# Second attention of a decoder layer: the norm of its own keys kept as a row of sums of squares and applied to the scores

## Chip, cores, metric

One Trainium2 chip, one core of it. The metric is the device time of one execution in microseconds (us). A TensorE matrix multiplication of 128 x 128 weights against up to 512 columns is a "matmul" here; PE is TensorE, DVE VectorE, ACT ScalarE, POOL GpSimd, and SP the engine that issues nearly all DMAs.

## What is computed

One decoder layer for 8 sequences of 100 tokens, width 1024, in fp32: a retention-style first attention, a second attention whose keys and values are those of a context of 722 rows followed by the layer's own 100 tokens, and a gated feed-forward net; a residual and a layer norm after each. What the change touches is the second attention (16 query heads, 4 key heads):

```python
q = (x @ wq).reshape(B, L, NUM_HEADS, HEAD_DIM)
k = (x @ wk).reshape(B, L, NUM_KV_HEADS, HEAD_DIM)
...
q = rms_norm(q, q_norm_w)
k = rms_norm(k, k_norm_w)
k_ctx = (h_ctx_kv @ wk_ctx).reshape(B, T, NUM_KV_HEADS, HEAD_DIM)
...
k_ctx = rms_norm(k_ctx, k_norm_w)
q = q * cos + rotate_half(q) * sin
k = k * cos + rotate_half(k) * sin
k_full = jnp.concatenate([k_ctx, k], axis=1)
...
scores = jnp.einsum('blhd,bmhd->bhlm', q, k_full) * scale + mask
probs = jax.nn.softmax(scores, axis=-1)
```

The norm of a key divides all 128 elements of it by one number, the root of their mean square. The rotation leaves the sum of squares of a key as it is. So this number may be applied to the key or to the key's row of scores.

## The kernel before

**Precision and layout.** A product in fp32 is three matmuls: each operand is split into a high and a low part, hi x hi, hi x lo, lo x hi (`mm3`, L85 to 88). `split2` (L63) makes the parts: a ScalarE copy (L67) and a VectorE subtraction (L68). Activations lie with features on the 128 partitions and tokens on the columns; a half is 4 sequences, 400 columns. `proj` (a loop over `mmw`) runs 24 matmuls of 400 columns into a bank of PSUM.

**Order.** The kernel is written as a program, and a list scheduler with a simulated time line then fixes the order of the instructions on each engine. Each engine runs its own queue in that order; an instruction whose input is not there holds all that stand behind it. That goes for SP too: a DMA that must wait for a buffer, or for another DMA's landing, holds the DMAs behind it.

**Stages** in the profile's time: first attention to about 440, its output projection to 605, the second attention's projections (L622 to 656) to 850, the attention over context and own keys (L661 to 764) to 1600, its output projection to 1730, the feed-forward net to 2450, the last norm to the end.

**The projections** go over 4 key heads, and for each over 6 units of weights (4 of queries, 1 of keys, 1 of values) and two halves. For a query or key unit: square the projection (L645), sum it over the partitions with GpSimd's all-reduce into `ss` (L125), rotate (`rope`, L133 to 137: two ScalarE copies, three VectorE operations), take the inverse root (`inv_root`: ScalarE Ln, Exp and Square at L113, L116, L118, and one Newton step on VectorE at L119 and L120, which leaves -2 times the root), multiply (L650), split into `d`, and store `d` to DRAM (`qd` or `kd`, L654). Values are turned by TensorE (`tokens_first`: a ScalarE copy `vt` at L145, the transposes at L148), split into `vs` and stored to `vd` (L642). The context keys and values of the first sequence's first two key heads are interleaved with this. The tiles `t`, `r`, `ss`, `sq` have two buffers here, `d` three.

**The attention** goes over 8 sequences and 4 key heads, 32 pairs. For each pair `context_keys` projects the 722 context rows in two parts, squares them (L604), sums them over the partitions into `ss` (tile kss, L605; its last 46 columns are set to 1 at L599), and writes that as a row to DRAM (L609). The unnormed keys, multiplied by the constant `kws` (the weight of the norm times -0.5 sqrt(128)), lie in `kall`; the 100 own keys, which are normed, are loaded behind them (L677). The row comes back from DRAM as a column, `rr` (L694: 128 partitions x 6), because the scores are laid out with keys on the partitions; six small operations (L696 to L703) make of it the factors `rk`. The scores are computed in 7 chunks of 128 keys, in the order 6, 5, 0, 1, 2, 3, 4. Chunk 6 holds own keys alone, chunk 5 82 rows of the context and 46 own keys. As each chunk leaves PSUM its rows are multiplied by a column of `rk`: chunks 0 to 4 on ScalarE (L722), chunks 5 and 6 on VectorE with the mask added (L718), where own keys have the factor 1: rows 82 to 127 of rk's column 5 are never written after the first 1.0, and chunk 6 uses the constant. Softmax, the product with the values and the store to `o2d` (L764) follow. Context values (`context_values`) are copied to `cvt` (L618) and turned by TensorE (L688).

At the change of sequence `load_context` loads the next context in 8 pieces `cs` (L588) and splits them into tiles `big`. These loads, the weights `w<-wcd` (L82), `kall`, `vall`, `q`, the row and `rr` all are issued by SP.

Of the kernel before, what the change touches and what calls it, by code (L numbers as in the profile page):

```python
# [8 lines left out]
F32 = mybir.dt.float32  # L9
FR = mybir.dt.float32r  # L10
AF = mybir.ActivationFunctionType
ALU = mybir.AluOpType
# [4 lines left out]
P = 128  # L17
B, T, D = 8, 100, 1024
# [4 lines left out]
SC, SH = 722, 362  # L23
SN = [SH, SC - SH]
NC = 7
ORDER = (6, 5, 0, 1, 2, 3, 4)
C5 = SC - 5 * P
# [4 lines left out]
NKV = 4  # L32
# [7 lines left out]
def decoder_layer(ctx, tc, xT, cT, w1, wo1, w2, wo2, wc, w3, wd, gw, qw, kw, trig, dec, mask, out):  # L40
# [18 lines left out]
    def bt(ap):  # L59
        return ap.rearrange("p (b t) -> p b t", b=NB)  # L60
# [49 lines left out]
    def inv_root(pool, ss, eps, n=N, pin=False):  # L110

        r = pool.tile([P, n], F32, tag="r0", name="r0")
        ln = nc.scalar.activation(r, ss, AF.Ln, bias=eps)  # L113
        if pin:
            tc.keep_in_program_order(ln)
        nc.scalar.activation(r, r, AF.Exp, scale=-0.5)  # L116
        q = pool.tile([P, n], F32, tag="r1", name="r1")
        nc.scalar.activation(q, r, AF.Square)  # L118
        nc.vector.scalar_tensor_tensor(q, ss, eps, q, ALU.add, ALU.mult)  # L119
        nc.vector.scalar_tensor_tensor(q, q, 3.0, r, ALU.subtract, ALU.mult)  # L120
        return q
# [31 lines left out]
    qd = dr.tile([NKV, 4, P, B, 2, T], FR, name="qd")  # L153
    kd = dr.tile([NKV, P, B, 2, T], FR, name="kd")
    vd = dr.tile([NKV, T, B, 2, P], FR, name="vd")
    o2d = dr.tile([B, P, NKV, 4, 2, T], FR, name="o2d")
    zd = dr.tile([2, P, KT, N], F32, name="zd")
    zd2 = dr.tile([2, P, KT, N], F32, name="zd2")
# [24 lines left out]
    eps_k = const(128e-6, "eps_k")  # L183
    rks = []
    for i in range(2):
        rk = cp.tile([P, 6], F32, name=f"rk{i}")
        nc.vector.memset(rk, 1.0)
        rks.append(rk)
    msk = cp.tile([P, 2, T], F32, name="msk")
    wts = cp.tile([P, 4], F32, name="wts")  # L190
    gws = cp.tile([P, 2], F32, name="gws")
# [4 lines left out]
    def load_constants(p, trg):  # L196
        dcy = p.tile([T, NH1, T], F32, name="dcy", bufs=1)
        nc.sync.dma_start(out=dcy, in_=dec)
        nc.sync.dma_start(out=msk, in_=mask)
        nc.sync.dma_start(out=wts[:, 0:2], in_=gw)  # L200
        nc.sync.dma_start(out=wts[:, 2:3], in_=qw)
        nc.sync.dma_start(out=wts[:, 3:4], in_=kw)

        nc.vector.tensor_scalar(gws, wts[:, 0:2], -8.0, None, ALU.mult)
        nc.vector.tensor_scalar(kws, wts[:, 3:4], -0.5 * math.sqrt(P), None, ALU.mult)
        nc.vector.tensor_scalar(tq, trg[:, 2:4], wts[:, 2:3], None, ALU.mult)
        nc.vector.tensor_scalar(tk, trg[:, 2:4], wts[:, 3:4], None, ALU.mult)
        for t in (tq, tk):
            sw = p.tile([P, T], F32, tag="vt", name="sw", bufs=1)
            nc.vector.tensor_copy(sw, t[:, 1])  # L210
            nc.vector.tensor_copy(t[0:P // 2, 1], sw[P // 2:P])
            nc.vector.tensor_copy(t[P // 2:P, 1], sw[0:P // 2])
        return dcy
# [361 lines left out]
    kapool = sbuf("ka", 2, "right")  # L575
    ka = kapool.__enter__()
    cz = []

    def load_context(b):

# [8 lines left out]
                split(z[k // QT][:, :, k % QT:k % QT + 2, :n], cs)  # L589
            cz.append(z)  # L590

    def context_keys(kv):

        kall = ka.tile([P, 2, SC + T], FR, tag="kall", name="kall")
        wk = load_ws(2 * kv)
        sq = ka.tile([P, SC], F32, tag="ksq", name="ksq", bufs=1)
        ss = ka.tile([P, 6 * P], F32, tag="kss", name="kss", bufs=1)
        row = dr.tile([6, P], F32, tag="row", name="row", bufs=2)
        nc.gpsimd.memset(ss[:, SC:], 1.0)  # L599

        def step(hf):
            n, at = SN[hf], slice(hf * SH, hf * SH + SN[hf])
            acc = proj(wk, cz[hf], n)
            nc.scalar.activation(sq[:, at], acc, AF.Square)  # L604
            nc.gpsimd.partition_all_reduce(ss[:, at], sq[:, at], P, RED.add)  # L605
            nc.scalar.activation(kall[:, 0, at], acc, AF.Copy, scale=kws)
            nc.vector.scalar_tensor_tensor(kall[:, 1, at], acc, kws, f32(kall[:, 0, at]), ALU.mult, ALU.subtract)
            if hf:
                nc.sync.dma_start(out=row.rearrange("c p -> (c p)")[None, :], in_=ss[0:1])  # L609
        return step, (kall, row)  # L610

    def context_values(kv):
# [10 lines left out]
    with sbuf("l2", 2) as p:  # L623
        for kv in range(NKV):
            for i0, i1 in ((0, 4), (4, 6)) if kv == 0 else ((0, 2), (2, 4), (4, 6)):
                if (kv, i0) == (0, 4):
                    load_context(0)
                ws = [load_w(w2[kv, i]) for i in range(i0, i1)]
                if (kv, i0) in ((1, 2), (2, 2)):
                    step, kept = context_keys(kv - 1)  # L630
                    early.append(kept)
                if (kv, i0) in ((1, 2), (2, 0), (2, 2), (3, 0)):
                    step(i0 == 0)
                for half in range(2):
                    bs = slice(half * NB, (half + 1) * NB)
                    for i in range(i0, i1):
                        acc = proj(ws[i - i0], z1[half], tag=acc_tag())
                        if i == 5:
                            tr = tokens_first(p, acc).rearrange("p (b d) -> p b d", b=NB)
                            vs = p.tile([T, NB, 2, P], FR, tag="vs", name="vs", bufs=1)  # L640
                            split2(vs[:, :, 0], vs[:, :, 1], tr)
                            nc.sync.dma_start(out=f32(vd[kv, :, bs]), in_=f32(vs))  # L642
                            continue
                        sq = p.tile([P, N], F32, tag="sq", name="sq")
                        nc.scalar.activation(sq, acc, AF.Square)  # L645
                        ss = all_red(p, sq, "ss")
                        tb = tq if i < 4 else tk
                        t = rope(p, acc, tb[:, 0], tb[:, 1])
                        r = inv_root(p, ss, eps_k)
                        nc.vector.scalar_tensor_tensor(  # L650
                            t, t, -0.5 if i < 4 else -0.5 * math.sqrt(P), r, ALU.mult, ALU.mult)
                        d = p.tile([P, NB, 2, T], FR, tag="d", name="d", bufs=3)
                        split2(d[:, :, 0], d[:, :, 1], bt(t))
                        nc.sync.dma_start(out=f32(qd[kv, i, :, bs] if i < 4 else kd[kv, :, bs]), in_=f32(d))  # L654
# [5 lines left out]
    with sbuf("cx", 2) as p, sbuf("c1", 1) as p1:  # L660
# [6 lines left out]
        for b in range(B):  # L667
            if b > 0:
                load_context(b)
            for kv in range(NKV):  # L670
                if early:
                    kall, row = early.pop(0)
                else:
                    step, (kall, row) = context_keys(kv)
                    step(0)
                    step(1)
                nc.sync.dma_start(out=f32(kall[:, :, SC:]), in_=f32(kd[kv, :, b]))  # L677
# [11 lines left out]
                    src = tr[0:rows, 0:(c1 - c0) * P].rearrange("p (c d) -> p c d", d=P)  # L689
                    split2(vall[0:rows, c0:c1, 0], vall[0:rows, c0:c1, 1], src)  # L690

                rr = p.tile([P, 6], F32, tag="rr", name="rr")
                with nc.allow_non_contiguous_dma("a row turned into a column"):
                    nc.sync.dma_start(out=rr, in_=row.rearrange("c p -> p c"))  # L694
                r0 = p.tile([P, 6], F32, tag="rr0", name="rr0")
                nc.scalar.activation(r0, rr, AF.Ln, bias=eps_k)  # L696
                nc.scalar.activation(r0, r0, AF.Exp, scale=-0.5)
                r1 = p.tile([P, 6], F32, tag="rr1", name="rr1")
                nc.vector.tensor_tensor(r1, r0, r0, ALU.mult)
                nc.vector.scalar_tensor_tensor(r1, rr, eps_k, r1, ALU.add, ALU.mult)  # L700
                rk = rks[kv % 2]
                nc.vector.scalar_tensor_tensor(rk[:, 0:5], r1[:, 0:5], 3.0, r0[:, 0:5], ALU.subtract, ALU.mult)
                nc.vector.scalar_tensor_tensor(rk[0:C5, 5:6], r1[0:C5, 5:6], 3.0, r0[0:C5, 5:6], ALU.subtract, ALU.mult)  # L703

                s = p1.tile([P, NC, N], F32, tag="s", name="s")
                mx = p.tile([P, N], F32, tag="mx", name="mx")
# [4 lines left out]
                for j, c in enumerate(ORDER):  # L711
                    rows, n, t0 = (R6, N6, T6) if c == 6 else (P, N, 0)
                    sp = bank("s")[0:rows, :n]
                    kh, kl = (kall[:, i, c * P:c * P + rows] for i in range(2))
                    mm3(bt(sp), kh, kl, q[:, :, 0, t0:], q[:, :, 1, t0:], True, True)
                    sc = s[0:rows, j, :n]
                    if c >= 5:
                        nc.vector.scalar_tensor_tensor(  # L718
                            bt(sc), bt(sp), rk[:, 5:6] if c == 5 else 1.0,
                            msk[0:rows, c - 5, None, t0:].to_broadcast([rows, 4, T - t0]), ALU.mult, ALU.add)  # L720
                    else:
                        nc.scalar.activation(sc, sp, AF.Copy, scale=rk[:, c:c + 1])  # L722
                        nc.vector.tensor_tensor(mx, s[:, 1] if j == 2 else mx, sc, ALU.max)
                    if j == 2:
                        m6 = part(mx, 6)
                        nc.vector.tensor_tensor(m6, m6, bt(s[0:R6, 0, :N6]), ALU.max)
# [348 lines left out]
```

## Time and profile before

| | us |
|---|---|
| median of 3 runs (lowest, highest) | 2515.79 (2514.77, 2517.98) |
| the profiled execution | 2517.7 |
| its span | 2515.9 |
| PE / DVE / ACT / POOL busy | 2465.4 / 1992.2 / 1343.5 / 481.2 |
| mean granted clock of TensorE | 0.993 of full |
| PE busy in 600 to 700, 700 to 800, 850 to 1000 | 89.72, 95.54, 149.49 |
| DVE busy in 600 to 700, 700 to 800, 850 to 1000 | 96.42, 91.33, 129.66 |
| all-reduce, one (56 in all of tile ss; 64 of tile kss) | 2.9; 2.7 |

How to read it: a busy time is the sum of an engine's instructions, the span runs from the first to the last of them. Line names such as L650 are lines of the kernel; "t<-t,r" is output and inputs by tile names. "DVE t L650" as a releaser means that a wait ended when VectorE's instruction of that line, on that tile, was done. The granted clock is what the chip's throttle lets TensorE have; at 0.5 each matmul takes twice its time.

### The profile page before, as it was taken

The numbers are of one execution on the slowest core, as the hardware profiler recorded it, in microseconds if no ns is written. First come the engines' busy times: TensorE is split into PE (matmuls) and PEld (weight loads), VectorE is DVE, ScalarE is ACT, GpSimd is POOL, SyncE is SP. The second block draws the span as 40 slices with busy tenths as digits, with TensorE's granted clock in tenths as the row PEclk, the third lists the DMA queues.
The fourth block names the chain that finished last, engine by engine and source line by source line (L and its number), as shares of the span: only waits on it lengthen the run. The fifth ranks groups of instructions, "written<-read, shape, count | busy, mean of one in ns | idle before, by whom it ended". The sixth has DMA issues, their size and how long they took to land.

```text
span 2515.9 us, 37158 instructions
## 1 busy us (share of the span) xinstructions
PE 2465.4 (98%) x14036; PEld 2442.0 (97%) x14036; DVE 1992.2 (79%) x3110; ACT 1343.5 (53%) x2264; POOL 481.2 (19%) x234
## 2 busy tenths in 40 slices
PE   8999999999899999999999999999999999999997
PEld 8999999999899999999999999999999999998997
DVE  7678876568989798899999999866987777666656
ACT  6667676335767565556566566533544544432221
POOL 0111111002645334433433433100000000000000
PEclk9999999999999999999999999999999999999999
DMA  7334445774444654554554554574455445388731
GB/s 240 110 110 127 136 144 187 239 266 148 144 152 133 207 175 142 178 166 151 169 176 144 166 192 135 189 273 152 145 181 192 159 160 167 127 302 311 250 102 53
DMA packets 224450, 433.96 MB, mean 172 GB/s; under 512 B 47338, under 2 KB 168042, under 8 KB 211854
## 3 DMA queue, kind: packets, MB, share of 16 engines
q1 hardware_dynamic: 223118, 427.39, 50.7%
q0 software_dynamic: 1152, 4.19, 1.1%
q8 instruction: 110, 1.80, 0.3%
q14 instruction: 70, 0.57, 0.1%
HBM read 322.18 MB, written 109.35 MB: 172 GB/s over the span
## 4 chain that ended last, share of the span: by engine, by line
PE 89%; DVE 6%; ACT 1%; DMA 1%; issue 1%; SPq 0%; DVEq 0%; ACTq 0%
PE a L88 18%; PE a L86 18%; PE a L87 18%; PE s L88 9%; PE s L87 9%; PE s L86 9%; PE v L88 2%; PE v L86 2%; PE v L87 2%; PE s L491 1%; PE s L688 1%; DVE r L120 1%; DVE r L119 1%; PE s L148 1%; DMA tp<-in_xT 1%
## 5 line engine op out<-in xcount | busy, mean ns | idle before, releaser
L86 PE MATMUL a<-big,w 128*128 128x400 f32 (+2 forms) x1808 | 611.4, 339 | 11.7 <-ACT big L67 7.4
L87 PE MATMUL a<-big,w 128*128 128x400 f32 (+2 forms) x1808 | 611.1, 338 | 0.0
L88 PE MATMUL a<-big,w 128*128 128x400 f32 (+2 forms) x1808 | 609.7, 338 | 0.0
L67 ACT CAST w<-wst 128x1024 fp32r<-128x1024 f32 (+1 forms) x231 | 239.2, 1038 | 389.4 <-PE s L88 130.7
L68 DVE TENSOR_TENSOR w<-wst,w 128x1024 fp32r<-128x1024 f32 (+1 forms) x231 | 281.0, 1218 | 117.0 <-ACT w L67 115.1
L86 PEld LDWEIGHTS a<-big,w 128*128 128x128 f32 x1808 | 341.3, 189 | 13.3 <-ACT big L67 7.7
L87 PEld LDWEIGHTS a<-big,w 128*128 128x128 f32 x1808 | 342.0, 189 | 1.3 <-DVE big L68 0.3
L88 PEld LDWEIGHTS a<-big,w 128*128 128x128 f32 x1808 | 342.0, 189 | 0.9 <-DVE w L68 0.2
L86 PE MATMUL s<-big,w 128*128 128x400 f32 x664 | 230.6, 347 | 0.1
L87 PE MATMUL s<-big,w 128*128 128x400 f32 x664 | 229.2, 345 | 0.0
L88 PE MATMUL s<-big,w 128*128 128x400 f32 x664 | 229.1, 346 | 0.0
L125 POOL PARTITION_ALL_REDUCE ss<-sq x56 | 161.1, 2881 | 336.3 <-DMA zd<-y 167.0
L605 POOL PARTITION_ALL_REDUCE kss<-ksq x64 | 173.2, 2706 | 116.4 <-ACT ksq L604 115.7
L86 PE MATMUL a<-z,w 128*128 128x400 f32 x488 | 168.6, 346 | 8.0 <-ACT r L118 4.3
L88 PE MATMUL a<-z,w 128*128 128x400 f32 x488 | 169.4, 348 | 0.7 <-DVE w L68 0.7
L87 PE MATMUL a<-z,w 128*128 128x400 f32 x488 | 169.4, 347 | 0.0
L87 PE MATMUL s<-z,w 128*128 128x400 f32 x400 | 139.1, 348 | 2.4 <-DVE z L68 2.4
L86 PE MATMUL s<-z,w 128*128 128x400 f32 x400 | 139.9, 350 | 0.0
L88 PE MATMUL s<-z,w 128*128 128x400 f32 x400 | 139.4, 348 | 0.0
L722 ACT ACTIVATE s<-s,rk 128x400 f32<-128x400 f32 x160 | 87.7, 591 | 91.9 <-DVE sm L742 65.5
L86 PEld LDWEIGHTS s<-big,w 128*128 128x128 f32 x664 | 124.6, 188 | 1.4 <-ACT w L67 0.4
L87 PEld LDWEIGHTS s<-big,w 128*128 128x128 f32 x664 | 124.6, 188 | 1.1
(330 smaller groups left out, 5650.9 us busy)
## 6 DMA issues: line engine op xcount, KB each, us to landing
wst<-in_w SPq DMA_DIRECT2D x135, 512.0 KB
w<-wcd SPq DMA_DIRECT2D x64, 1024.0 KB
wst<-in_wo SPq DMA_DIRECT2D x64, 512.0 KB
hd<-h SPq DMA_DIRECT2D x12, 1400.0 KB
wst<-in_wd SPq DMA_DIRECT2D x64, 256.0 KB
big<-o1d SPq DMA_DIRECT2D x16, 800.0 KB
qd<-d SPq DMA_DIRECT2D x32, 400.0 KB
q<-qd SPq DMA_DIRECT2D x32, 400.0 KB
```

The costliest lines, as they stand in the source:

```text
L67: nc.scalar.copy(hi, src)
L68: nc.vector.tensor_tensor(lo, src, f32(hi), ALU.subtract)
L86: nc.tensor.matmul(acc, lh, rh, start=start, stop=False, skip_group_check=chain)
L87: nc.tensor.matmul(acc, lh, rl, start=False, stop=False, skip_group_check=chain)
L88: nc.tensor.matmul(acc, ll, rh, start=False, stop=stop, skip_group_check=chain)
L119: nc.vector.scalar_tensor_tensor(q, ss, eps, q, ALU.add, ALU.mult)
L120: nc.vector.scalar_tensor_tensor(q, q, 3.0, r, ALU.subtract, ALU.mult)
L125: nc.gpsimd.partition_all_reduce(y, x, P, op)
L148: nc.tensor.transpose(tr[0:T, b * P:(b + 1) * P], vt[:, b * T:(b + 1) * T], ident)
L491: nc.tensor.matmul(bt(o)[:, b], vv[:, b * P:(b + 1) * P], pf[:, b], start=True, stop=True)
L605: nc.gpsimd.partition_all_reduce(ss[:, at], sq[:, at], P, RED.add)
L722: nc.scalar.activation(sc, sp, AF.Copy, scale=rk[:, c:c + 1])
```

## The change

- The key units of the projections no longer take the inverse root nor multiply by it (L113 to L120 and L650 for 8 units: 4 key heads x 2 halves). The rotation tables of keys, `tk`, are built with `kws` instead of the bare weight, so that own keys have the same factor as the context's.
- The sums of squares of own keys (`ss`, one row of 400 values for half the sequences) are stored to a new DRAM tensor `ksd`.
- The row of a pair is now one of two fixed DRAM tensors of 7 x 128 elements: 722 sums of the context, 100 of own keys, and a constant tail of 74 that is written once at the start. For each pair a DMA copies 100 values from `ksd` to the row, DRAM to DRAM. The memset at L599 goes.
- `rr` and `rk` have 7 columns; one VectorE operation makes all of `rk` instead of two; chunk 6 is multiplied by its column like the others.

Matmuls and all-reduces stay as they are. The diff:

```diff
--- before.py
+++ after.py
@@ -153,6 +153,7 @@
     qd = dr.tile([NKV, 4, P, B, 2, T], FR, name="qd")
     kd = dr.tile([NKV, P, B, 2, T], FR, name="kd")
     vd = dr.tile([NKV, T, B, 2, P], FR, name="vd")
+    ksd = dr.tile([NKV, B, T], F32, name="ksd")
     o2d = dr.tile([B, P, NKV, 4, 2, T], FR, name="o2d")
     zd = dr.tile([2, P, KT, N], F32, name="zd")
     zd2 = dr.tile([2, P, KT, N], F32, name="zd2")
@@ -183,9 +184,7 @@
     eps_k = const(128e-6, "eps_k")
     rks = []
     for i in range(2):
-        rk = cp.tile([P, 6], F32, name=f"rk{i}")
-        nc.vector.memset(rk, 1.0)
-        rks.append(rk)
+        rks.append(cp.tile([P, NC], F32, name=f"rk{i}"))
     msk = cp.tile([P, 2, T], F32, name="msk")
     wts = cp.tile([P, 4], F32, name="wts")
     gws = cp.tile([P, 2], F32, name="gws")
@@ -204,7 +203,7 @@
         nc.vector.tensor_scalar(gws, wts[:, 0:2], -8.0, None, ALU.mult)
         nc.vector.tensor_scalar(kws, wts[:, 3:4], -0.5 * math.sqrt(P), None, ALU.mult)
         nc.vector.tensor_scalar(tq, trg[:, 2:4], wts[:, 2:3], None, ALU.mult)
-        nc.vector.tensor_scalar(tk, trg[:, 2:4], wts[:, 3:4], None, ALU.mult)
+        nc.vector.tensor_scalar(tk, trg[:, 2:4], kws, None, ALU.mult)
         for t in (tq, tk):
             sw = p.tile([P, T], F32, tag="vt", name="sw", bufs=1)
             nc.vector.tensor_copy(sw, t[:, 1])
@@ -575,6 +574,9 @@
     kapool = sbuf("ka", 2, "right")
     ka = kapool.__enter__()
     cz = []
+    rows2 = [dr.tile([1, NC * P], F32, name=f"row{i}") for i in range(2)]
+    for row in rows2:
+        nc.sync.dma_start(out=row[:, SC + T:], in_=onem[0:1, 0:NC * P - SC - T])
 
     def load_context(b):
 
@@ -589,14 +591,15 @@
                 split(z[k // QT][:, :, k % QT:k % QT + 2, :n], cs)
             cz.append(z)
 
-    def context_keys(kv):
+    def context_keys(b, kv):
+
 
         kall = ka.tile([P, 2, SC + T], FR, tag="kall", name="kall")
         wk = load_ws(2 * kv)
         sq = ka.tile([P, SC], F32, tag="ksq", name="ksq", bufs=1)
-        ss = ka.tile([P, 6 * P], F32, tag="kss", name="kss", bufs=1)
-        row = dr.tile([6, P], F32, tag="row", name="row", bufs=2)
-        nc.gpsimd.memset(ss[:, SC:], 1.0)
+        ss = ka.tile([P, SC], F32, tag="kss", name="kss", bufs=1)
+        row = rows2[kv % 2]
+        nc.sync.dma_start(out=row[:, SC:SC + T], in_=ksd[kv, b][None, :])
 
         def step(hf):
             n, at = SN[hf], slice(hf * SH, hf * SH + SN[hf])
@@ -606,7 +609,7 @@
             nc.scalar.activation(kall[:, 0, at], acc, AF.Copy, scale=kws)
             nc.vector.scalar_tensor_tensor(kall[:, 1, at], acc, kws, f32(kall[:, 0, at]), ALU.mult, ALU.subtract)
             if hf:
-                nc.sync.dma_start(out=row.rearrange("c p -> (c p)")[None, :], in_=ss[0:1])
+                nc.sync.dma_start(out=row[:, :SC], in_=ss[0:1])
         return step, (kall, row)
 
     def context_values(kv):
@@ -627,7 +630,7 @@
                     load_context(0)
                 ws = [load_w(w2[kv, i]) for i in range(i0, i1)]
                 if (kv, i0) in ((1, 2), (2, 2)):
-                    step, kept = context_keys(kv - 1)
+                    step, kept = context_keys(0, kv - 1)
                     early.append(kept)
                 if (kv, i0) in ((1, 2), (2, 0), (2, 2), (3, 0)):
                     step(i0 == 0)
@@ -646,9 +649,11 @@
                         ss = all_red(p, sq, "ss")
                         tb = tq if i < 4 else tk
                         t = rope(p, acc, tb[:, 0], tb[:, 1])
-                        r = inv_root(p, ss, eps_k)
-                        nc.vector.scalar_tensor_tensor(
-                            t, t, -0.5 if i < 4 else -0.5 * math.sqrt(P), r, ALU.mult, ALU.mult)
+                        if i < 4:
+                            r = inv_root(p, ss, eps_k)
+                            nc.vector.scalar_tensor_tensor(t, t, -0.5, r, ALU.mult, ALU.mult)
+                        else:
+                            nc.sync.dma_start(out=ksd[kv, bs].rearrange("b t -> (b t)")[None, :], in_=ss[0:1])
                         d = p.tile([P, NB, 2, T], FR, tag="d", name="d", bufs=3)
                         split2(d[:, :, 0], d[:, :, 1], bt(t))
                         nc.sync.dma_start(out=f32(qd[kv, i, :, bs] if i < 4 else kd[kv, :, bs]), in_=f32(d))
@@ -671,7 +676,7 @@
                 if early:
                     kall, row = early.pop(0)
                 else:
-                    step, (kall, row) = context_keys(kv)
+                    step, (kall, row) = context_keys(b, kv)
                     step(0)
                     step(1)
                 nc.sync.dma_start(out=f32(kall[:, :, SC:]), in_=f32(kd[kv, :, b]))
@@ -689,18 +694,17 @@
                     src = tr[0:rows, 0:(c1 - c0) * P].rearrange("p (c d) -> p c d", d=P)
                     split2(vall[0:rows, c0:c1, 0], vall[0:rows, c0:c1, 1], src)
 
-                rr = p.tile([P, 6], F32, tag="rr", name="rr")
+                rr = p.tile([P, NC], F32, tag="rr", name="rr")
                 with nc.allow_non_contiguous_dma("a row turned into a column"):
-                    nc.sync.dma_start(out=rr, in_=row.rearrange("c p -> p c"))
-                r0 = p.tile([P, 6], F32, tag="rr0", name="rr0")
+                    nc.sync.dma_start(out=rr, in_=row.rearrange("o (c p) -> (o p) c", p=P))
+                r0 = p.tile([P, NC], F32, tag="rr0", name="rr0")
                 nc.scalar.activation(r0, rr, AF.Ln, bias=eps_k)
                 nc.scalar.activation(r0, r0, AF.Exp, scale=-0.5)
-                r1 = p.tile([P, 6], F32, tag="rr1", name="rr1")
+                r1 = p.tile([P, NC], F32, tag="rr1", name="rr1")
                 nc.vector.tensor_tensor(r1, r0, r0, ALU.mult)
                 nc.vector.scalar_tensor_tensor(r1, rr, eps_k, r1, ALU.add, ALU.mult)
                 rk = rks[kv % 2]
-                nc.vector.scalar_tensor_tensor(rk[:, 0:5], r1[:, 0:5], 3.0, r0[:, 0:5], ALU.subtract, ALU.mult)
-                nc.vector.scalar_tensor_tensor(rk[0:C5, 5:6], r1[0:C5, 5:6], 3.0, r0[0:C5, 5:6], ALU.subtract, ALU.mult)
+                nc.vector.scalar_tensor_tensor(rk, r1, 3.0, r0, ALU.subtract, ALU.mult)
 
                 s = p1.tile([P, NC, N], F32, tag="s", name="s")
                 mx = p.tile([P, N], F32, tag="mx", name="mx")
@@ -716,7 +720,7 @@
                     sc = s[0:rows, j, :n]
                     if c >= 5:
                         nc.vector.scalar_tensor_tensor(
-                            bt(sc), bt(sp), rk[:, 5:6] if c == 5 else 1.0,
+                            bt(sc), bt(sp), rk[0:rows, c:c + 1],
                             msk[0:rows, c - 5, None, t0:].to_broadcast([rows, 4, T - t0]), ALU.mult, ALU.add)
                     else:
                         nc.scalar.activation(sc, sp, AF.Copy, scale=rk[:, c:c + 1])
```

## Prediction

> **What bounds the kernel now.** I read the profile in the order whole span, chain, stages, waits. The page first:
>
> ```profile
> PE 2465.4 (98%) x14036; PEld 2442.0 (97%) x14036; DVE 1992.2 (79%) x3110; ACT 1343.5 (53%) x2264; POOL 481.2 (19%) x234
> PE 89%; DVE 6%; ACT 1%; DMA 1%; issue 1%; SPq 0%; DVEq 0%; ACTq 0%
> ```
>
> TensorE is busy 98% of the span, and the change leaves every matmul as it is. So nothing can be won but TensorE's idle time (2515.9 - 2465.4, some 50 us) and time at a lower granted clock. The 6% of the chain on VectorE say where to look. The busy time by stretch shows which stage it is (columns: length, then busy us of PE, weight load, DVE, ACT, POOL, then granted clock, DMA share, GB/s):
>
> ```profile
> 630.00:640.00 10.00, 5.67 (x24) 5.37 (x23) 10.00 (x13) 6.47 (x14) 6.03 (x3) 0.83 0.41 155
> 670.00:680.00 10.00, 7.54 (x35) 7.20 (x35) 9.93 (x15) 8.90 (x17) 5.72 (x2) 0.84 0.62 198
> 710.00:720.00 10.00, 7.22 (x34) 6.88 (x33) 9.81 (x17) 5.76 (x12) 1.35 (x1) 0.83 0.45 157
> 730.00:760.00 30.00, 30.00 (x168) 30.00 (x167) 27.92 (x40) 20.94 (x42) 18.57 (x8) 1.00 0.43 149
> 850.00:860.00 10.00, 9.49 (x51) 9.46 (x52) 4.76 (x16) 3.52 (x11) 0.69 (x2) 0.83 0.85 325
> ...
> 1000.00:1150.00 150.00, 150.00 (x910) 149.05 (x909) 135.41 (x240) 88.52 (x173) 59.18 (x31) 1.00 0.54 173
> ```
>
> The second attention's projections run from 605 to 850. Up to about 720 VectorE has no free time and TensorE waits; from 720 to 830 TensorE is full. The context pairs (870 to 1600) have no TensorE wait at all. TensorE's waits between 590 and 860 (us in total, times, longest):
>
> ```profile
> PE a L86 <- ACT r L118: 4.3, 1, 4.3
> PE s L148 <- ACT vt L145: 4.2, 3, 2.8
> PE a L86 <- DMA w<-wcd: 2.5, 1, 2.5
> PE s L87 <- DVE z L68: 2.4, 1, 2.4
> PE s L688 <- ACT cvt L618: 1.9, 1, 1.9
> PE a L86 <- ACT w L67: 1.4, 1, 1.4
> PE a L88 <- DVE w L68: 0.7, 1, 0.7
> ```
>
> **A wait costs more than itself.** In the trace the gaps of 2.4, 4.3, 2.5, 2.8 and 1.9 us in this stage are each followed by 3.41 us at a granted clock of 0.5 (hence the 0.83 in the rows above, 3.41 x 0.5 / 10 below 1). Each such stretch loses 3.41 x 0.5 = 1.7 us of matmul work. Gaps of 1.4 us and less (five over the span) have none. So I price a stall of 1.9 us or more with 1.7 us on top.
>
> The Trainium skill weighs differently here ("TensorE: Matmul & The Clock Gate", Part 1 and "HAM oscillation"): the clock falls after an idle window of about 3.4 us. By that rule only the 4.3 us gap would be followed by half clock, and each term of 1.7 us below would be 0; the rows decide otherwise.
>
> **The change part by part.**
>
> *Norm of own keys taken out of the projections (8 units: 4 key heads x 2 halves).* Per unit go three ScalarE activations (0.63 + 0.54 + 0.54 = 1.7 us by the rows of L113, L116, L118) and three VectorE operations, L119, L120 and L650. Their means in this stage are 0.66, 0.85 and 0.91 us, but that contains single ones stretched to 1.6 to 2.5 us while GpSimd's all-reduce is starting or ending; that stretch will hit a neighbour instead. The undisturbed pitch is 0.49, 0.55 and 0.55, so 1.6 us per unit (2.4 by the means). The all-reduces all stay. Only the units inside the VectorE-bound part pay: both key units of head 0 and the first of head 1 lie before 720. 3 x 1.6 = **4.8 us**. Below: 2 units, 3.2. Above: everything that TensorE loses after the first key unit (655), that is 2.5 + 0.35 + 1.4 + 0.7 + 2.8 = 7.7 us of gaps and two half-clock stretches, 3.4: 11.1. The other five units lie where TensorE is full: 0, and they pay only if TensorE would otherwise run dry, which no row shows. Without that cover they would be worth 5 x 1.6 = 8 us more.
>
> *The end of the projections.* At 848.6 TensorE waits 1.9 us for one copy of the context's values (L618). ScalarE's queue shows why (start, us; in brackets idle before and what ended it):
>
> ```profile
> 847.66 0.59 ACT L67 CAST vs<-s 100x512 fp32r<-100x512 f32 x1 [5.96 <-DMA vd<-vs]
> 849.06 0.30 ACT L696 ACTIVATE rr<-rr,eps_k 128x6 f32<-128x6 f32 x1 [0.81 <-DMA rr<-row]
> ...
> 850.02 0.44 ACT L618 COPY cvt<-a 128x362 f32<-128x362 f32 x1
> ```
>
> The copy stands behind a cast that waits for a DMA and behind the Ln of the keys' norms that waits for its column. In the changed program's order on ScalarE, this copy stands ahead of both. So the gap and its half clock go: 1.9 + 1.7 = **3.6 us** (0 if a neighbour takes the place, 4.3 with the 0.7 us gap at 834).
>
> *The weight load in head 0.* The 2.5 us wait for w<-wcd is a load issued at 670.8, just after the first kd<-d at 670.4. In the changed order it stands behind a new ksd copy, behind kall<-kd (which waits for kd's landing, some 2.3 us) and behind the second kd<-d. But kd is ready 4 to 6 us earlier, because the Ln, Exp, Square and the product are gone from its chain, and the load is first used 18 matmuls (3.3 us) later. The two shifts about cancel: 0, between -1.5 and +2.5 (a loss). A DRAM-to-DRAM copy is in no row of the trace. Its landing lies between that of the 3 KB rr<-row in a quiet stretch (2.1 us from issue to use) and in the busiest (7.4, below); I take 2.4.
>
> *DRAM to DRAM.* SP issues 42 more DMAs: 2 constant tails, 8 ksd<-ss and 32 row<-ksd, at 0.24 to 0.37 us (the rows of row<-kss and rr<-row): 10 to 16 us of SP. SP has time: its queue waits 105 us for d alone between 590 and 860. What matters is the wait. Row<-ksd overwrites the row buffer from which rr<-row has just been issued, so SP must hold until that one has landed. From issue of rr to the start of its Ln, where ScalarE stood waiting, the trace gives 2.1 to 2.7 us, at most 4.5 in the pairs and 7.4 at 841.6. Behind the held SP in mid-stage stand w<-wcd (used 25 us or more after), q, kall, vall (each with more than 5 us) and, at a change of batch, the context loads:
>
> ```profile
> 1186.32 0.24 SPq L609 DMA_DIRECT2D row<-kss  x1
> 1188.61 0.37 SPq L694 DMA_DIRECT2D rr<-row  x1
> 1190.04 1.20 SPq L588 DMA_DIRECT2D cs<-in_cT  x2
> 1192.40 0.34 SPq L82 DMA_DIRECT2D w<-wcd  x1
> 1193.81 0.37 SPq L588 DMA_DIRECT2D cs<-in_cT  x1
> ```
>
> In the changed order row<-ksd stands ahead of the 4th load in the second batch, the 5th in the third and the 6th in the others. There rr (1188.6) has landed by about 1191.3, while the 6th load goes at 1193.8: no delay. The split tiles of those loads are ready 2.2 to 4.0 us before TensorE needs them, but the last only 0.5 to 0.9 us. In the second batch the load would slip from 906.5 to about 910, 3.5 us against 3.6. I take 0; bounds 0 and -3.
>
> The Trainium skill speaks against this part ("DMA: Bandwidth & Descriptors", "Anatomy of one DMA"): a DMA queue does not wait, the issuing sequencer does, and a copy has a fixed cost of about 2 us. By that figure SP would be held some 2 us per pair, which the slack above still covers.
>
> *The small operations of the pairs.* The GpSimd memset (L599, 0.14 us) and one VectorE operation (L703, 0.146 us) go, 32 of each: 4.7 us of VectorE, beside a full TensorE: 0. The all-reduce now takes over the memset's wait for row<-kss (62 us in all): no change. The last chunk, first in order, now needs rk. Rk ends 17 to 31 us before that chunk's evacuation in pairs 1 to 30, 6.6 and 6.3 us in the first and last: hidden. One more column makes rr 896 instead of 768 elements: 128/768 of 2.4 us, 0.4 us, hidden too.
>
> **Sum.** 4.8 + 3.6 = 8.4 us from the profiled execution's 2517.7 (span 2515.9 and 1.8 around it) gives 2509.3. The median of the runs shown is 2515.8, 1.9 lower; from it the sum gives 2507.4. I take **2508.5**.
>
> **Rivals.**
> 1. *The relief is taken up.* The stall of 2.8 us is a copy behind VectorE's queue, that of 2.5 us a DMA; stalls that move rather than shrink leave 3.2 us or less in the middle, and a new wait at the end of the stage returns its 3.6. Gain 0 to 5: 2511 to 2516. For it: five of eight units lie where TensorE is full. Against it: VectorE at 10.0 of 10 us.
> 2. *Slower: SP held in front of the context loads.* If rr lands 4.5 us after its issue (seen) at a change of batch instead of 2.7, the last tiles are late by 4.5 - 2.4 = 2.1 us at each of seven changes, and a gap of 2.1 us brings 1.7 of half clock: 7 x 3.8 = 27 us at the most, 14.7 without the clock. With 14.7, less the 8.4: 2515.8 + 6.3 = 2522. It decides from the landing time on at which slack (2.2 to 4.0 us) is used up. Against it: in the steady batches three issues stand between rr and row<-ksd.
> 3. *The change doesn't do what it says:* the key chain still waits, now in SP's queue. Kall<-kd and w<-wcd queue behind ksd<-ss and its landing, and the gap at 674 grows by 2.5 us: gain 8.4 - 2.5 - 1.7 = 4.2, 2511.6.
>
> **How the numbers follow.** About 0.2% (5 us) is what a measurement of this kernel can tell from no change; faster means below 2510.8. Forecast 0.50 (2501 to 2510.8: the upper bounds 11.1 + 4.3 give 15.4, 2500.4). Rivals 1 and 3 together 0.33, 2511 to 2517, nearly all within 0.2%. Rival 2: 0.17, of which the part up to 2517.5 is in the range. Range 2501 to 2517.5.
>
> **What would show it.** Right: the VectorE-bound part ends some 5 us earlier by the same matmul, the window around 711 at clock 1.0, no wait for cvt near 845, no TensorE wait from 870 on. Wrong: a TensorE wait for big or L67 at 900 to 1500 (rival 2), a longer wait for w<-wcd (rival 3), or an unchanged number of half-clock stretches before 860. What can upset it all: another order of the instructions in the last stage, where 3.2 us of gap and 6.8 us at half clock (2316) may move.

## The result, and the profile after

The changed kernel takes 2539.89 us (median of 6 runs, 2534.44 to 2543.29), the kernel before 2516.39 (6 runs): ratio on record 1.0086, 95% interval 1.0076 to 1.0097. By the medians it is 23.5 us slower; 2508.5 had been forecast, 2501 to 2517.5 as the range. The page of the changed kernel (busy times, then the chain):

```profile
PE 2475.9 (97%) x14036; PEld 2447.6 (96%) x14036; DVE 1993.1 (78%) x3052; ACT 1332.3 (52%) x2240; POOL 476.0 (19%) x202
PE 50%; DVE 7%; DMA 3%; ACT 2%; POOL 2%; issue 2%; SPq 0%; DVEq 0%; ACTq 0%; POOLq 0%
```

The same 14036 matmuls. The shares of the chain of what ended last cannot be set directly against the 89% of before: here it could be followed back only to 849 us, and its shares add up to 66% of the span, against 98% before. Of what it covers TensorE has about three quarters (50 of 66) instead of nine tenths (89 of 98); pieces on VectorE, DMA and GpSimd have come in. Both traces have the same number of TensorE records, and in much the same sequence (line and tiles agree for 11537 of them), so the n-th start of one can be set against the n-th of the other. That shows at what time the 23 us arise (worked out from the two traces):

```
n-th matmul   before    after   difference   where
 3300         578.46   579.76     +1.30      before the projections
 4500         817.17   813.68     -3.49      projections, middle over
 4800         872.60   868.06     -4.54      projections over
 6150        1095.95  1094.40     -1.55      context pairs
 6300        1120.73  1122.74     +2.01
 6900        1219.82  1226.35     +6.53
 7500        1318.93  1329.52    +10.59
 8100        1418.20  1434.52    +16.32
 8700        1516.91  1538.76    +21.86
 9150        1592.53  1615.44    +22.91      context pairs over
13950        2482.98  2506.05    +23.07      end
```

The projections won 5.8 us. The context pairs lost 27.5, in steps of 3.6 to 5.8, one at each change of sequence from the fourth sequence on (smaller ones before and after), and next to nothing between the steps. In this stretch (870 to 1600) the two kernels' busy times are, first before, then after (columns as in the prediction):

```profile
870.00:1600.00 730.00, 730.00 (x4410) 724.92 (x4409) 667.66 (x1159) 446.66 (x852) 291.90 (x150) 1.00 0.52 167
```

```profile
870.00:1600.00 730.00, 716.20 (x4252) 707.00 (x4251) 651.52 (x1083) 426.47 (x823) 279.13 (x117) 0.99 0.49 158
```

TensorE was full before and now stands idle for 14 us; in the same time it does 158 fewer matmuls, and no other engine is busier. TensorE's waits there (us in total, times, longest), of which the kernel before has none:

```profile
PE a L86 <- DVE kall L610: 9.6, 6, 1.9
PE s L86 <- ACT s L726: 1.4, 5, 0.7
PE a L86 <- DMA big<-o2d: 1.0, 1, 1.0
PE s L693 <- ACT s L726: 0.9, 2, 0.5
PE s L86 <- DVE vall L68: 0.8, 1, 0.8
```

The first is a wait for a bank of PSUM that VectorE empties late (L610, the low part of the context keys). One of the six, on TensorE and then on VectorE (start, length, operation):

```profile
1311.05 1.18 PE L693 MATMUL s<-ident,cvt 128*128 128x128 f32 x6
...
1314.71 0.67 PE L86 MATMUL a<-big,w 128*128 128x360 f32 x1 [1.80 <-DVE kall L610]
```

```profile
1309.84 1.89 DVE L727 TENSOR_TENSOR mx<-mx,s 128x400 f32<-128x400 f32 x1
...
1313.59 0.56 DVE L765 SCALAR_TENSOR_TENSOR ofs<-v,r 128x400 f32<-128x400 f32 x1
1314.07 0.58 DVE L610 SCALAR_TENSOR_TENSOR kall<-a,kws,kall 128x362 fp32r<-128x362 f32 x1
1315.06 0.58 DVE L610 SCALAR_TENSOR_TENSOR kall<-a,kws,kall 128x360 fp32r<-128x360 f32 x1
```

VectorE has no gap here; L610 is merely behind other work in its queue. Five of the six gaps are of 1.6 to 1.9 us, and each of these is followed by 3.4 or 6.8 us at a granted clock of 0.5. There a matmul of 360 columns starts every 0.30 us instead of every 0.165, so that 3.4 us lose 1.5 us of work (the prediction reckoned with 1.7). The 14 us of idle time and six times 1.5 us make up 23 of the 27.5 us; the rest was not traced to single waits.

Where does a new order come from? GpSimd's all-reduces at a change of sequence, first before, then after (ksq: keys of the next pair, in two halves; sm, mx: sum and maximum of the softmax of the pair in work):

```profile
1293.96 2.60 POOL L125 PARTITION_ALL_REDUCE mb<-sm  x1 [10.63 <-DVE sm L742]
1298.20 3.04 POOL L605 PARTITION_ALL_REDUCE kss<-ksq  x1 [1.63 <-ACT ksq L604]
1305.89 1.73 POOL L125 PARTITION_ALL_REDUCE mb<-mx  x1 [4.65 <-DVE mx L723]
1307.52 2.46 POOL L605 PARTITION_ALL_REDUCE kss<-ksq  x1
```

```profile
1301.12 2.60 POOL L608 PARTITION_ALL_REDUCE kss<-ksq  x1 [12.45 <-ACT ksq L607]
1307.15 2.60 POOL L125 PARTITION_ALL_REDUCE mb<-sm  x1 [3.43 <-DVE sm L746]
1309.66 2.46 POOL L608 PARTITION_ALL_REDUCE kss<-ksq  x1
1315.30 1.47 POOL L125 PARTITION_ALL_REDUCE mb<-mx  x1 [3.19 <-DMA row<-kss]
```

Before, the second half of the next keys is reduced after the maximum; now both halves come ahead of it. After its first ten pairs the kernel before repeats four pairs as S k X k, k S X k, S k X k, S k X k (k keys, X maximum, S sum); the changed kernel has S k X k in all from its eighth pair on. The letters hide that the halves differ: with a and b for the first and second half of one pair's keys, the kernel before has S a X b (and a S X b), the changed one a S b X. So the scheduler has laid out the pairs anew. One reading, which no run tests by itself: with both halves of the next keys projected early, TensorE has fewer matmuls left that it could run while VectorE splits the new context (8 tiles at 0.9 us).

The traces show another part of what the new order costs. A VectorE instruction can take much longer while an all-reduce runs: the L727 at 1309.84 above takes 1.89 us, those after it 0.56, and it starts 0.2 us after the all-reduce of the second half at 1309.66. In four of the five gaps such an instruction stands six places ahead of the L610 that TensorE waits for. Between 870 and 1620 the VectorE instructions that take over 0.6 us more than the median of their like number 42 in the kernel before and 50 in the changed one, and all of them overlap an all-reduce.

### The profile page after: what moved, and what is told of

Its sections match the earlier page's. It is cut to its first block, busy times and chain, and to the rows that moved or that the text cites. A ratio compares the mean times of both kernels' runs of the same rounds, so it can differ in the third digit from the quotient of the medians.

```text
span 2539.5 us, 37153 instructions
## 1 busy us (share of the span) xinstructions
PE 2475.9 (97%) x14036; PEld 2447.6 (96%) x14036; DVE 1993.1 (78%) x3052; ACT 1332.3 (52%) x2240; POOL 476.0 (19%) x202
## 4 chain that ended last, share of the span: by engine, by line
PE 50%; DVE 7%; DMA 3%; ACT 2%; POOL 2%; issue 2%; SPq 0%; DVEq 0%; ACTq 0%; POOLq 0%
PE a L86 10%; PE a L88 10%; PE a L87 10%; PE s L88 6%; PE s L86 6%; PE s L87 6%; DVE sm L746 1%; DMA cs<-in_cT 1%; DVE pl L68 1%; POOL kss L608 1%; DVE mx L727 1%; DMA rr<-row 1%; PE v L88 1%; PE v L86 1%; PE v L87 1%
```

## The experiments

Theory O: the order is what costs. Theory S, the prediction's rival 2: SP, held by the copies, is late with the context loads. Times are medians in us. Each ratio is to the kernel before, measured on the same chip; it is an estimate with a 95% interval and lies within 0.1% of the quotient of the medians.

**Chunk 6 with the constant again** (all of the rest changed; the own keys in chunk 6 are then left unnormed):

```diff
-  bt(sc), bt(sp), rk[0:rows, c:c + 1],
+  bt(sc), bt(sp), rk[0:rows, c:c + 1] if c == 5 else 1.0,
```

> The changed kernel, but chunk 6 is multiplied by the constant 1 again instead of a column of rk (the norm of the own keys in chunk 6 is left out). All copies, waits of SP and the 7 columns stay. Theory O (order): what costs the time is that chunk 6 now depends on rk, which makes the scheduler lay out the 32 pairs in another order (GpSimd's queue is S k X k in all pairs, S the all-reduce of the sum, X that of the maximum, k those of the keys; before, every fourth pair was k S X k); with the constant the queue is as before, so the time falls by about 28 us to 2507 to 2513. Theory S (SP held by the copies in front of the context loads): the copies are all there, so the time stays at 2535 to 2543.

2512.82, ratio 0.9985 (0.9976 to 0.9995). No gap of 1.4 us or more between 870 and 1600. All copies are in it, and SP is held by them for longer (53.6 us from 870 to 1600, against 44.0 in the changed kernel, below): theory S falls here.

**The kernel before, chunk 6 reading a column of rk:**

```diff
-  rk = cp.tile([P, 6], F32, name=f"rk{i}")
+  rk = cp.tile([P, NC], F32, name=f"rk{i}")
...
-  bt(sc), bt(sp), rk[:, 5:6] if c == 5 else 1.0,
+  bt(sc), bt(sp), rk[0:rows, c:c + 1],
```

> The kernel before, but rk has a seventh column of ones which chunk 6 reads as its factor: only the dependence of chunk 6 on rk is added, no DMA, no copy, no change in the projections. Theory O: the order of the pairs becomes that of the changed kernel (S k X k throughout), and the time rises by 15 to 28 us, to 2531 to 2544. Theory S: nothing that holds SP is added, 2514 to 2519.

2542.32, ratio 1.0099 (1.0082 to 1.0116). This one operand makes the whole loss.

**No copies, and four rows:**

```diff
-  nc.sync.dma_start(out=row[:, SC + T:], in_=onem[0:1, 0:NC * P - SC - T])
+  nc.sync.dma_start(out=row[:, SC:SC + P], in_=onem[0:1, 0:P])
+  nc.sync.dma_start(out=row[:, SC + P:], in_=onem[0:1, 0:NC * P - SC - P])
...
-  nc.sync.dma_start(out=row[:, SC:SC + T], in_=ksd[kv, b][None, :])
```

> The changed kernel without its 32 copies from DRAM to DRAM per pair (own keys get a constant factor from a constant tail of the row; the sums of squares of own keys are stored but not used). Order of the pairs as in the changed kernel. Theory O: 2533 to 2543. Theory S: SP is no longer held, the time falls to 2507 to 2515.

```diff
-  rows2 = [... for i in range(2)]
+  rows2 = [... for i in range(4)]
...
-  row = rows2[kv % 2]
+  row = rows2[kv]
```

> The changed kernel with four row tensors instead of two, so that a copy need not wait for the landing of the rr that was issued just before. Theory O: 2533 to 2543, as changed. Theory S: the wait is gone, so the time falls by 10 us or more, to 2530 or less.

2539.07 (1.0083, 1.0064 to 1.0102) and 2543.73 (1.0101, 1.0084 to 1.0118): by the intervals neither can be told from the changed kernel. The hold of SP is real, as its own queue's waits in the changed kernel show (870 to 1600), but nothing is won without it:

```profile
SPq L602 <- DMA rr<-row: 44.0, 27, 2.9
```

**A column of ones that nothing writes.** Is it the dependence on rk, or only the form of the operation?

```diff
+  one = ka.tile([P, 1], F32, tag="one", name="one", bufs=1)
+  nc.vector.memset(one, 1.0)
...
-  bt(sc), bt(sp), rk[:, 5:6] if c == 5 else 1.0,
+  bt(sc), bt(sp), rk[:, 5:6] if c == 5 else one[0:rows],
```

> The kernel before, with chunk 6 multiplied by a column of ones in a tile of its own, which nothing writes after the start: the operation takes its factor from a tile instead of a constant, but chunk 6 does not depend on rk. The scheduler lays out the pairs as in the second experiment all the same. If the order alone counts (theory O without the dependence), the time is that of the second experiment, 2539 to 2546. If the chip's wait of chunk 6 for rk counts, the time stays at 2514 to 2519.

2538.33, ratio 1.0087 (1.0067 to 1.0107). Theory O stands, but without the dependence: the first two expectations were wrong about how the order comes to change. It is enough that the factor is read from a tile. VectorE's operation itself (before, then this run; 870 to 1600) is 65 ns longer by that, 2 us over 32 pairs:

```profile
L718 DVE SCALAR_TENSOR_TENSOR s<-s,msk 54x216 f32<-54x216 f32 x30 | 11.0, 368 | 0.3
```

```profile
L720 DVE SCALAR_TENSOR_TENSOR s<-s,one,msk 54x216 f32<-54x216 f32 x29 | 12.5, 433 | 0.9
```

**The keys' way out of PSUM with priority** (changed kernel):

```diff
+  with tc.high_priority():
       nc.scalar.activation(kall[:, 0, at], acc, AF.Copy, scale=kws)
       nc.vector.scalar_tensor_tensor(kall[:, 1, at], acc, kws, ...)
```

> The changed kernel, with the two operations that take the projected context keys out of PSUM (L609, L610) given high priority with the scheduler, so that they stand earlier in ScalarE's and VectorE's queues. Theory O says that TensorE's gaps at the changes of sequence are waits for a bank that L610 frees late: they should go or shrink under 1.4 us, with their half clock, and the time falls by 8 to 25 us, to 2515 to 2532. If the gaps come from too much VectorE work at the change of sequence whatever its order, they stay: 2535 to 2543.

2541.61 (1.0099, 1.0084 to 1.0114). A miss. The wait for kall did shrink (0.74 us at five places), but one for the banks of the scores took its place:

```profile
PE s L86 <- ACT s L727: 6.3, 6, 1.1
PE a L86 <- DVE kall L611: 5.0, 6, 1.3
```

Gaps of 0.4, 1.1 and 0.7 us within 3 us (from 1311 on) were followed by half clock as one of 2 us is. So L610 alone was not the cause but the place where the queue showed.

**The projections alone** (before, norm of own keys left out):

```diff
-  r = inv_root(p, ss, eps_k)
-  nc.vector.scalar_tensor_tensor(t, t, -0.5 if i < 4 else ..., r, ALU.mult, ALU.mult)
+  if i < 4:
+      r = inv_root(p, ss, eps_k)
+      nc.vector.scalar_tensor_tensor(t, t, -0.5, r, ALU.mult, ALU.mult)
```

> The kernel before without the norm of own keys in the projections (left out altogether; no sums stored, no copies, factor 1 in chunk 6). The pairs are laid out much as before. This prices the projections alone: by the prediction 8.4 us less, 2505 to 2510; by the first experiment (3.4 us less, with the copies in) 2510 to 2514; the difference between the two is what the stores of the sums and copies cost in the projections.

2510.84 (0.9981, 0.9972 to 0.9991): 5.0 less, at the lower end of the second of the ranges given. The first experiment won 3.4; the difference is within the intervals of the two.

**Context values with priority** (changed kernel):

```diff
+  with tc.high_priority():
       vt = context_values(kv)
       ... (the transposes and splits of vt)
```

> The changed kernel with the projection and turning of the context values given high priority with the scheduler, which gives a third order of the pairs (GpSimd's queue is S k k X at each change of sequence). If the loss belongs to one order and not to the work, another order has another loss: outside 2535 to 2543. If any order with this work loses the same, 2535 to 2543. A size cannot be told beforehand; if its gaps of 1.4 us and more at the changes of sequence are gone, 2510 to 2520.

2557.09 (1.0157, 1.0142 to 1.0173): the same work in a third order loses 41 us.

**Holding back the next keys by hand** (changed kernel, and the second experiment's):

```diff
-  acc = proj(wk, cz[hf], n)
+  if scored and hf and kv == 0:
+      with tc.issue_after(scored[-1].ins):   # third score chunk
+          acc = proj(wk, cz[hf], n)
+  else:
+      acc = proj(wk, cz[hf], n)
```

> The changed kernel with one thing told to the scheduler: at a change of sequence, TensorE issues the second half of the next pair's key projection behind the third score chunk of the pair in work, which is about how the kernel before had it. Work, operands, copies and waits are those of the changed kernel. If the loss is in the order at the changes of sequence and in nothing else, the gaps of 1.4 us and more between 1000 and 1600 go and the time is near that of the first experiment: 2509 to 2517. If what the change computes needs the time in any order, 2533 to 2543.

> The second experiment's kernel (before, with chunk 6 reading a column of ones of rk; 2542) with the same instruction to the scheduler as in the ninth. By the theory of the order, back to 2513 to 2522; otherwise 2535 to 2545.

2561.87 (1.0185, 1.0170 to 1.0199) and 2555.65 (1.0158, 1.0144 to 1.0172). Both missed: 46 and 40 us over the kernel before. The wait for kall has gone, others came (ninth experiment):

```profile
PE s L86 <- DVE vall L68: 18.1, 8, 3.7
PE s L86 <- ACT s L734: 8.4, 10, 2.5
```

The scheduler has built another order around the one constraint (in the ninth S a X b in all later pairs, without the a S X b of before), and it is worse. That one half of one projection decides was thus not shown.

**Two ways back to the pattern of before, with the change in.** In the first, ScalarE applies the factor of chunk 6 after the operation with the constant (the factor is negative, so the mask of chunk 6 is turned over with it; all other work is there). In the second, the two copies of the context values swap engines:

```diff
-  bt(sc), bt(sp), rk[0:rows, c:c + 1],
+  bt(sc), bt(sp), rk[0:rows, c:c + 1] if c == 5 else 1.0,
...
+  if c == 6:
+      nc.scalar.activation(sc, sc, AF.Copy, scale=rk[0:rows, c:c + 1])
```

> The changed kernel, all of its work done; only chunk 6 is multiplied by the constant 1 with the mask added, as before, and its factor from rk is then applied by ScalarE in place (32 more ScalarE operations of about 0.4 us). The scheduler lays out the 32 pairs as in the first experiment and as before (GpSimd k S X k at each change of sequence). If the order is all that costs, 2510 to 2516, faster than the kernel before; if using the factor in chunk 6 costs in any order, 2530 or more.

```diff
-  copy = nc.scalar.copy if hf == 0 else nc.vector.tensor_copy
+  copy = nc.scalar.copy if hf == 1 else nc.vector.tensor_copy
```

> The changed kernel with the two halves of the copy of the context values swapped between ScalarE and VectorE (first half VectorE, second half ScalarE; nothing is added or taken away). Chunk 6 keeps its factor from rk in one VectorE operation. The scheduler's order of the pairs has GpSimd at k S X k at each change of sequence, as before. If the order is all that costs, 2509 to 2518; if it is the form of chunk 6's operation on the chip, 2530 or more.

2511.80 (0.9983, 0.9974 to 0.9992) and 2510.47 (0.9980, 0.9971 to 0.9989). (The pair with k S X k is one in four, the one after the change of sequence; the expectations put it at the change.) The last computes all that the changed kernel does, with the same operand in chunk 6, and is some 29 us faster than it and 5 us faster than the kernel before. Neither the operand nor the swap by itself is left as a rival: the eleventh swaps nothing, the twelfth keeps the operand. TensorE from 870 to 1600 in the twelfth:

```profile
870.00:1600.00 730.00, 729.71 (x4404) 724.38 (x4403) 663.12 (x1127) 442.59 (x845) 276.18 (x120) 1.00 0.52 166
```

It is full again, with copies, the 7 columns and the factor in place. Its 3052 VectorE instructions, as many as the changed kernel's and of the same kinds, are busy for 1977.2 us instead of 1993.1, and 37 instead of 50 are stretched beside an all-reduce.

Over all 14 runs GpSimd's queue tells the two groups apart. The five that repeat S a X b, a S X b, S a X b, S a X b (the kernel before, the first, seventh, eleventh and twelfth experiments) take 2510 to 2516 us; the nine with any other order take 2538 to 2562, whatever they compute. The stretched instructions do not explain it all: the ninth, the slowest, has only 34.

## Why the prediction was wrong, step by step

- **Where it failed:** "The small operations of the pairs", with its "The last chunk, first in order, now needs rk. [...] hidden". The slack given there was there in the changed kernel too (rk ends 8.3 us ahead in the first pair, 21 to 39 in the others), and the fifth experiment shows that the dependence is not the point. But the step, and the sum with it, priced this edit inside the order of before. The scheduler made another order of the pairs because of this operand, and that cost 27.5 us where 0 stood; the sign "no TensorE wait from 870 on" failed with it. "Another order" was named at the end, for the last stage alone. The order of the changed program could be read before any run: no k S X k among its pairs after the eighth, against one in four. It had been read in the projections and for the context loads, not for the pairs.
- **The norm out of the projections, middle:** forecast 4.8; between the 3300th and the 4500th matmul 1.30 + 3.49 = 4.8. Right in sum, but in part by luck. It was priced as VectorE work saved; in the traces it is made up of the stalls at 700 that went, the one at 711 that shrank to 0.6 us, and two that grew (at 631 from 4.3, at 675 from 2.5 us). One half-clock stretch (1.5 us) fell away by chance: the gap of 2.4 us at 606 stayed and was not followed by one this time. The waits of the changed kernel, 590 to 860:

```profile
PE a L86 <- ACT r L118: 5.6, 1, 5.6
PE a L86 <- DMA w<-wcd: 3.3, 1, 3.3
...
PE s L86 <- DVE s L722: 1.7, 1, 1.7
```

- **The end of the projections:** forecast 3.6 (1.9 + 1.7; by the measured pace of the half clock 1.9 + 1.5 = 3.4), measured 4.54 - 3.49 = 1.1. The stall of 1.9 us on L618 and its half clock went, but waits of 1.1 (the copy's second half on VectorE) and 1.7 us (the last line above) took the place: the bound "0 if a neighbour takes the place" was nearer.
- **The weight load in head 0:** within its bounds: 3.3 us against 2.5, a loss of 0.8, contained in the 4.8 above. (In the upper bound of the middle, 11.1, the gaps are 7.3 us and not 7.7: the trace has no gap of 0.35 there.)
- **DRAM to DRAM:** 0, as forecast, within some 5 us; the third and fourth experiments show it. The section of the Trainium skill that the prediction takes a fixed cost of about 2 us from ("DMA: Bandwidth & Descriptors", "Anatomy of one DMA") measures DMAs that GpSimd issues. These are issued by SP, which was held 1.6 us a time (44.0 us in 27 waits), 2.9 at most. **Rival 2** had the right side and nearly the right size (7 changes of sequence, up to 27 us), but by luck, for the cause was another.
- **Rival 1** (the relief is taken up, gain 0 to 5) fits what the runs in the pattern of before show of the projections: a gain of 3.4, 3.8 and 5.2 us (first, eleventh, twelfth experiments), not 8.4. **Rival 3** came true in small, with the 0.8 us at w<-wcd.
- Not settled: why this operand turns the scheduler to another order, and which of the moved instructions makes that order the slower one. The sixth, ninth and tenth experiments tried single places and each moved the wait elsewhere; the instructions stretched beside an all-reduce are a candidate that no run tests by itself.

## What to carry to other kernels

Where a scheduler orders the instructions, an edit is not a local one: price it only after the order of the changed program has been set against that of before in every stage, above all in the stage with the most instructions, and let a stage that is full but has no reserve count as a risk of loss. If such an edit loses time in a stage whose work it hardly touches, look for a change of no weight (here two copies that swap engines) that brings the old order back, before giving up the edit. And add up the gaps of TensorE that lie close together: they can bring the half clock as one does.

## What the runs showed of the hardware

The half clock came after less idle time, and less surely, than "a stall of 1.9 us or more". Over the 14 traces, from 500 to 2400 us, TensorE's gaps (of 0.3 us and more, those within a stretch of 5 us added up) were followed by a stretch at granted clock 0.5:

```
idle us      followed / all
under 1.5       2 / 152
1.5 to 2       22 / 40
2 to 3         38 / 53
3 and more     43 / 43
```

One gap of 2.77 us (704 in the twelfth experiment) had none, one of 1.56 us (1114 in the changed kernel) had one; of two gaps of 1.57 us in the second experiment the one at 1213 had none, the one at 1412 had one. The Trainium skill ("TensorE: Matmul & The Clock Gate", "What's actually happening") has the gate watch a free-running window of about 3.4 us; that the same gap is followed at one time and not at another agrees with a free-running window. That a window's worth of idle time is needed does not: half of it, 1.5 to 2 us, was enough in 22 of 40 cases.

The half clock costs less than half of its time: matmuls of 360 and 400 columns start every 0.300 and 0.333 us in it, every 0.165 and 0.182 at full clock (medians, before and changed kernel), 1.8 times and not twice. And a VectorE instruction that meets an all-reduce of GpSimd can take 1.89 us instead of 0.56.
